# Copies of queries to the other partitions by DMA within SBUF, transfers to every second partition, and VectorE's exps in every group of the seven-tile blocks

## The chip, the cores and the metric

The kernel runs on one core of a Trainium2 chip. The metric is the device time of one launch in microseconds; a run's number is the median of several executions. The profile is of one execution and has its own time.

## What is computed

The reference is four graph layers on 3,327 nodes with 128 features; each adds its result to its input and normalizes. Nearly all the time is in layer 0, an attention with 8 heads' worth of features per slot and 128 slots. Cut to what matters:

```python
q = (x @ Wq.T).reshape(d, n, h)        # d = 128 slots, n = 3327 nodes, h = 8
k = (x @ Wk.T).reshape(d, n, h)
v = (x @ Wv.T).reshape(d, n, h)
a = jnp.einsum('dnh,dmh->dnm', q, k) * scale
a = a + adj + adj                      # the same matrix stands for both encodings
a = jax.nn.softmax(a, axis=2)
out = jnp.einsum('dnm,dmh->dnh', a, v)
```

So for every slot there is a 3,327 x 3,327 matrix of scores with a contraction over 8 features only, an exponential of each, and a product with 9 columns (8 values and a one for the sum). The other three layers are products of the adjacency matrix with 128 or 256 columns.

## The kernel before, in words

**Preparation** (to 339 us) projects x to queries, keys and values. Queries and keys are split into a high and a low part of TensorE's float32r[...]: 32 rows of contraction. They are stored in the DRAM scratches `q_s` and `k_s`, 16 rows each (8 high, 8 low), one row of all slots behind the other.

**Attention** (339 to 10,020 us) is tiled thus. There are 7 stretches of 476 queries (`CW`). For each of them the keys are taken in four parts (`KBS`): two of seven tiles of 128 keys, two of six. That makes 28 blocks. In a block the 128 slots are gone through in 32 groups of four (`GROUP`), 896 groups in all. PSUM holds the scores of one slot and block in three sets `sc0`, `sc1`, `sc2` of 3, 2 and 2 tiles (2, 2 and 2 in a six-tile block). At a block's first slot the transposed edges are put into PSUM; each further slot adds its score less that of the slot before, so the edges stay there. That is why the contraction has 64 rows: 32 for the slot's keys and queries and 32 for the earlier slot's keys (`back` = 1) and negated queries.

A group's sets have twelve places, 0 to 11: four slots, three sets each. At each place TensorE computes the set's scores (L610) and ScalarE their exps (L618). Tiles alternate between the two halves of TensorE's rows: even tiles use partitions 0 to 63 of `kt` and `qt`, odd tiles partitions 64 to 127. So `qt` holds the same queries in both halves. In three of four groups (`on_vector`) the last set of the first slot gets its exps from VectorE (`vector_exp`: L574, L575, L577 and five times L580). A group is weighed by the values (`weigh`, L636) while the next group's scores are computed. `PLACES` says after which places the tiles are weighed: for six-tile blocks one tile at every second place, for seven-tile blocks by a list of its own for each of four successive groups; `FIRST` serves the first group of a block.

Order of the work: TensorE, ScalarE, VectorE and GpSimd run in the order in which the program is written. VectorE's smaller steps go through a list `vec`, from which `vector_work` takes them by a running account of estimated microseconds (`clock`), so that they come between the sets. SP only issues loads, in order; before one it waits for the semaphores of the buffer that it overwrites and for the DMA that used the same completion semaphore last (there are eight).

At the start of group n (`prepare`), SP issues the loads for group n+2 (`load_heads`): three into `qt` (L469) and eight into `kt` (L476), both with three buffers; every second group also the values `vs` (L511), and every eighth a piece `ai` of adj (L184) for the later layers. VectorE then completes the queries of group n+1 (`copy_queries`): L499 and L500 write the negated queries of the earlier slots to partitions 32 to 63, L501 copies partitions 0 to 63 to 64 to 127. The loads put the 16 rows of `q_s` or `k_s` on 16 neighbouring partitions.

**The last layers** (10,020 us to the end) are not touched.

The functions that the diff touches, with the line numbers of the profile:

Of the kernel before, what the change touches and what calls it, by code (L numbers as in the profile page):

```python
# [19 lines left out]
P = 128  # L20
GROUP = 4
# [29 lines left out]
def kernel(ctx: ExitStack, tc: tile.TileContext, x, adj, wq, wk, wv, wo,  # L51
# [14 lines left out]
    nc = tc.nc  # L66
    N, D = x.shape
    HD = wq.shape[0]
    H = HD // D
# [175 lines left out]
    with tc.tile_pool(name="pw", bufs=1) as pw, tc.tile_pool(name="pa", bufs=2) as pa, \  # L245
# [155 lines left out]
        one = pw.tile([1, 512], F32, name="one")  # L401
        nc.vector.memset(one, 1.0)
        nc.sync.dma_start(out=klead_s, in_=zero)
        for row in (0, 2 * H):
            nc.sync.dma_start(out=klead_s[row:row + 1, :], in_=one)
        nc.sync.dma_start(out=k_s[:, SLOTS:RS], in_=zero[0:2 * H, :])

# [1 line left out]
    def attention():  # L409
        with tc.tile_pool(name="acc", bufs=1) as accp, tc.tile_pool(name="kq", bufs=3) as kq, \  # L410
# [31 lines left out]

            SETS = {7: [(0, 3), (3, 2), (5, 2)], 6: [(0, 2), (2, 2), (4, 2)]}

            def on_vector(g):

                return g % 4 != 0

            PLACES = {7: ((0, 2, 4, 4, 7, 7, 9), (0, 0, 3, 7, 7, 10, 10), (0, 0, 3, 6, 6, 9, 9), (0, 0, 3, 6, 7, 10, 10)),
                      6: ((0, 2, 4, 6, 8, 10),) * 4}

            FIRST = {7: (4, 4, 5, 7, 7, 10, 10), 6: (4, 4, 7, 7, 10, 10)}

            def load_heads(b, g):


                c0, kb = blocks[b]
                k0, nt = KBS[kb]  # L460
                ns = [(nt + 1) // 2, nt // 2]
                kt = kq.tile([P, GROUP, 4 * P], F32R, name="kt")
                qt = kq.tile([P, GROUP, CW], F32R, name="qt")
                qf = qt.bitcast(F32)
                kf = kt.bitcast(F32)

                d = g * GROUP
                for row, a, n in ((0, 0, 16), (16, H, H), (24, 0, H)):
                    nc.sync.dma_start(out=qf[row:row + n],  # L469
                                      in_=flat_ap(q_s, a * RS + c0 + d * N, [[RS, n], [N, GROUP], [1, CW]]))  # L470
                for back in range(2):
                    j = 1 if back and g == 0 else 0
                    for rg in range(2):
                        for u in range(2):
                            row = 64 * rg + 32 * back + 16 * u
                            nc.sync.dma_start(  # L476
                                out=kf[row:row + 16, j:, 0:ns[rg] * P],
                                in_=flat_ap(k_s, (d + j - back) * N + (k0 + (ns[0] if rg else 0)) * P,
                                            [[RS, 16], [N, GROUP - j], [1, ns[rg] * P]]))
                if g == 0:  # L480
                    for rg in range(2):
                        nc.sync.dma_start(out=kf[64 * rg + 32:64 * rg + 64, 0, 0:ns[rg] * P],
                                          in_=klead_s[:, 0:ns[rg] * P])
                    nc.vector.memset(qf[32:64, 0], 0.0)
                    u = c0 // SUPER
                    cut = min(CW, (u + 1) * SUPER - c0)
                    for uu, a, n in ((u, 0, cut), (u + 1, cut, CW - cut)):
                        for row, part in ((0, 0), (8, 1), (16, 1), (24, 0)):
                            if n:
                                nc.sync.dma_start(  # L490
                                    out=qf[32 + row:33 + row, 0, a:a + n],
                                    in_=flat_ap(lead_s[uu], part * SUPER + c0 + a - uu * SUPER, [[SUPER, 1], [1, n]]))
                return kt, qt

            def copy_queries(b, g):
                qt = heads[b, g][1]
                qf = qt.bitcast(F32)
                before = heads[b, g - 1][1].bitcast(F32)[0:32, GROUP - 1] if g else qf[32:64, 0]
                return [(0.9, None, lambda: nc.vector.tensor_scalar(qt[32:64, 1:], qf[0:32, 0:GROUP - 1], -1.0, None, ALU.mult)),  # L499
                        (0.4, None, lambda: nc.vector.tensor_scalar(qt[32:64, 0], before, -1.0, None, ALU.mult)),  # L500
                        (1.2, None, lambda: nc.vector.tensor_copy(qt[64:128], qf[0:64]))]  # L501

            def tile_at(nt, i):

# [41 lines left out]
            def prepare(b, d):  # L546

                n = b * NHG + d // GROUP
                if d % GROUP == 0:
                    while any(of is None for _, of, _ in vec):  # L550
                        vec.pop(0)[2]()
                    if n + 2 < len(groups):
                        heads[groups[n + 2]] = load_heads(*groups[n + 2])
                    if n + 1 < len(groups):
                        values[groups[n + 1]] = load_values(*groups[n + 1])
                    while stores:
                        store(*stores.pop(0))
                    background(n)


                if d % GROUP == 1 - on_vector(d // GROUP) and n + 1 < len(groups):
                    vec.extend(copy_queries(*groups[n + 1]))
                if d % GROUP == 3:
                    background_work(n)
# [29 lines left out]
            def exponents(b, d, si):  # L594
                kb = blocks[b][1]
                nt = KBS[kb][1]
                t0, n = SETS[nt][si]
                s = sc[si]
                if d == 0:
                    for i in range(n):  # L600
                        tl = tile_at(nt, t0 + i)[2]
                        for j, (q0, w) in enumerate(subs):
                            nc.tensor.matmul(s[:, i, q0:q0 + w], lhsT=edges[b][0:w, j, tl * P:(tl + 1) * P],
                                             rhs=ident[0:w, 0:w], is_transpose=True,
                                             start=(j == 0), stop=True, skip_group_check=True)
                kt, qt = heads[b, d // GROUP]
                k = d % GROUP
                for i in range(n):
                    rg, pos, _ = tile_at(nt, t0 + i)
                    nc.tensor.matmul(s[:, i, 0:CW], lhsT=kt[64 * rg:64 * rg + 64, k, pos * P:(pos + 1) * P],  # L610
                                     rhs=qt[64 * rg:64 * rg + 64, k, :],
                                     start=False, stop=True, skip_group_check=True)
                e = ex.tile([P, (3, 2, 2)[si], CW], F32, tag=f"e{si}", name=f"e{si}", bufs=(6, 7, 8)[si])
                if on_vector(d // GROUP) and (d % GROUP, si) == (0, 2):
                    vector_exp(e[:, 0:n, :], s[:, 0:n, 0:CW], (b, d // GROUP))
                    clock[1] += 1.2
                else:
                    nc.scalar.activation(e[:, 0:n, :], s[:, 0:n, 0:CW], AF.Exp, scale=2.0)  # L618
                for i in range(n):
                    es[b, d, t0 + i] = e[:, i, :]  # L620
                if d % (2 * GROUP) == 0 and d // (2 * GROUP) < len(subs) and si == len(SETS[nt]) - 1 \
                        and b + 1 < len(blocks):
                    load_edges(b + 1, d // (2 * GROUP))
# [39 lines left out]
            with tc.manual_schedule(engines={mybir.EngineType.PE, mybir.EngineType.Activation,  # L663
                                             mybir.EngineType.Pool, mybir.EngineType.DVE}):
                for j in range(len(subs)):
                    load_edges(0, j)
                for n in range(2):
                    heads[groups[n]] = load_heads(*groups[n])
                for _, _, step in copy_queries(*groups[0]):
                    step()  # L670
                values[groups[0]] = load_values(*groups[0])
                for b, d in steps:
                    prepare(b, d)
                    for si in range(len(SETS[KBS[blocks[b][1]][1]])):
                        vector_work(b)
                        exponents(b, d, si)
                        if queue:
                            at = PLACES[len(queue_of)][d // GROUP % 4] if d >= GROUP else FIRST[len(queue_of)]
                            for _ in range(at.count(place)):
                                weigh(*queue.pop(0))  # L680
                        place += 1
                    if d % GROUP == GROUP - 1:
                        while queue:
                            weigh(*queue.pop(0))
                        queue_of = [(b, d // GROUP, r) for r in range(KBS[blocks[b][1]][1])]
                        queue, place = list(queue_of), 0
                while queue:
                    weigh(*queue.pop(0))
                while stores:
                    store(*stores.pop(0))  # L690
# [558 lines left out]
```

## Time and profile before

| | |
|---|---|
| median of 3 runs | 10,783.05 us (10,782.16 to 10,786.95) |
| profiled execution, its own time | 10,792.99 us |
| its span | 10,791.2 us |
| TensorE (PE) busy | 10,545.2 us, 98% |
| ScalarE (ACT) busy | 9,680.6 us, 90% |
| VectorE (DVE) busy | 8,700.0 us, 81% |
| GpSimd (POOL) busy | 1,852.8 us, 17% |
| DMA packets | 995,965, 1,516.25 MB, mean 141 GB/s |
| SP's queue (q1) | 1,371.76 MB, its packets take 78.7% of 16 engines' span |

How to read it: busy time is the union of an engine's instructions. A group of instructions is given by its line, engine, operation and shapes, with count, busy time, mean duration of one, and the idle time of the engine before them with what ended it. Where instructions overlap in the engine's pipeline, the mean of one is longer than the spacing. The forty digits of a row are tenths of busy time in forty equal slices. TensorE's ends are modelled, so its 98% does not mean that it works at its peak.

### The profile page before, as it was taken

To read this page: it belongs to the slowest core of one execution; us is meant where nothing else is said; L and a number is where in the kernel's file an instruction comes from. 1 tells how busy PE (TensorE), PEld (TensorE's weight loads), DVE (VectorE), ACT (ScalarE), POOL (GpSimd) and SP (SyncE) were. 2 spreads that over 40 slices of the span, in tenths; PEclk is the share of its full clock that TensorE was granted. 3 is DMA by queue.
4 is the path that set the end of the run, shared out by engine and by line. 5 is a ranking of instruction groups with operands and counts; after the bars stand their busy time and mean duration, and the time that the engine had idled before them with its cause. 6 is when DMAs were issued, how large, how long until landed. Compare 5 with 4: busy or idle time off the path is not lost. (4 is left out here: it accounts for less than half of the span.)

```text
span 10791.2 us, 203132 instructions
## 1 busy us (share of the span) xinstructions
PE 10545.2 (98%) x76941; PEld 4103.4 (38%) x76941; DVE 8700.0 (81%) x9695; ACT 9680.6 (90%) x10559; POOL 1852.8 (17%) x2742
## 2 busy tenths in 40 slices
PE   8899999999999999999999999999999999999999
PEld 5333333333333333333333333333333333333779
DVE  6688998889988899888899788998889877788412
ACT  3799999999999999999999999999999999999400
POOL 0111122111221122211122111121112100001200
PEclk9899999999999999999999999999999999999999
DMA  7888888888888888888888788888888888888676
GB/s 251 156 129 124 131 139 136 128 126 129 136 140 125 125 132 135 137 125 128 129 139 137 116 123 122 125 132 129 129 128 126 124 120 118 115 114 121 214 281 246
DMA packets 995965, 1516.25 MB, mean 141 GB/s; under 512 B 203368, under 2 KB 813474, under 8 KB 981164
## 3 DMA queue, kind: packets, MB, share of 16 engines
q1 hardware_dynamic: 897750, 1371.76, 78.7%
q0 software_dynamic: 79616, 116.88, 4.9%
q8 instruction: 624, 10.22, 0.5%
q10 hardware_dynamic: 17620, 14.49, 0.4%
q14 instruction: 355, 2.90, 0.1%
HBM read 1371.86 MB, written 130.35 MB: 139 GB/s over the span
## 5 line engine op out<-in xcount | busy, mean ns | idle before, releaser
L618 ACT ACTIVATE e<-sc 128x952 f32<-128x952 f32 (+1 forms) x10080 | 9458.5, 1090 | 247.6 <-PE sc L610 216.5
L636 PE MATMUL o<-e,v_pad 128*32 128x476 f32 (+1 forms) x46592 | 5621.3, 573 | 38.2 <-DVE acc L649 25.5
L610 PE MATMUL sc<-qt,kt 64*128 64x476 f32 x23296 | 4470.2, 438 | 113.8 <-ACT e L618 63.6
L610 PEld LDWEIGHTS sc<-qt,kt 64*128 64x128 f32 x23296 | 2166.0, 184 | 4415.6 <-ACT e L618 3840.0
L580 DVE SCALAR_TENSOR_TENSOR e<-e,ey 128x952 f32<-128x952 f32 x2016 | 2319.7, 1151 | 66.4
L515 POOL COPY v_pad<-vs 128x192 f32<-128x192 f32 (+1 forms) x896 | 606.7, 702 | 7666.8 <-DMA vs<-v_img 5875.9
L636 PEld LDWEIGHTS o<-e,v_pad 128*32 128x32 f32 (+1 forms) x46592 | 1045.1, 108 | 1967.2 <-issue 1931.9
L574 DVE TENSOR_SCALAR ey<-sc 128x952 int32<-128x952 f32 x672 | 772.1, 1149 | 624.6 <-PE sc L610 615.1
L501 DVE CAST qt<-qt 64x1904 fp32r<-64x1904 f32 x896 | 1041.5, 1162 | 30.4
L499 DVE TENSOR_SCALAR qt<-qt 32x1428 fp32r<-32x1428 f32 x896 | 809.0, 903 | 140.4 <-DMA qt<-q_s 109.5
L234 POOL DMA_DIRECT2D adjT_s<-at x1352 | 853.5, 638 | 232.6 <-DMA adjT_s<-at 168.2
L580 DVE SCALAR_TENSOR_TENSOR e<-ey 128x952 f32<-128x952 f32 x672 | 773.5, 1151 | 23.3
L580 DVE SCALAR_TENSOR_TENSOR e<-e,et 128x952 f32<-128x952 f32 x672 | 774.1, 1152 | 20.7
L1085 PE MATMUL bank<-y,eT 128*128 128x128 f32 (+1 forms) x4056 | 473.9, 276 | 0.4 <-DVE h L1207 0.4
L1085 PEld LDWEIGHTS bank<-y,eT 128*128 128x128 f32 (+1 forms) x4056 | 465.3, 192 | 5.7 <-DVE h L1207 0.6
L577 DVE TENSOR_SCALAR ey<-ey 128x952 int32<-128x952 int32 x672 | 447.1, 665 | 23.3
L575 DVE TENSOR_SCALAR et<-ey 128x952 int32<-128x952 int32 x672 | 443.1, 659 | 22.5
L500 DVE TENSOR_SCALAR qt<-qt 32x476 fp32r<-32x476 f32 x896 | 385.7, 430 | 6.2 <-DMA qt<-lead_s 3.2
L649 DVE TENSOR_TENSOR acc<-o,acc 128x476 f32<-128x476 f32 x231 | 150.4, 651 | 248.8 <-PE o L636 247.6
L1045 ACT ACTIVATE rstd<-mv,eps 128x1 f32<-128x1 f32 x104 | 30.4, 293 | 265.2 <-DVE mv L1043 265.2
L656 POOL DMA_DIRECT2D o_s<-acc x308 | 238.7, 779 | 30.0 <-DVE acc L649 20.2
L647 DVE COPY acc<-o 128x476 f32<-128x476 f32 x77 | 50.1, 650 | 136.4 <-PE o L636 135.8
(151 smaller groups left out, 2357.8 us busy)
## 6 DMA issues: line engine op xcount, KB each, us to landing
kt<-k_s SPq DMA_DIRECT2D x5320, 96.0 KB
kt<-k_s SPq DMA_DIRECT2D x1764, 128.0 KB
eT<-adjT_s SPq DMA_DIRECT2D x78, 1664.0 KB
qt<-q_s SPq DMA_DIRECT2D x896, 119.0 KB
qt<-q_s SPq DMA_DIRECT2D x1792, 59.5 KB
vs<-v_img SPq DMA_DIRECT2D x224, 224.0 KB
adjT_s<-at POOLq DMA_DIRECT2D x1352, 32.0 KB, 6.3
vs<-v_img SPq DMA_DIRECT2D x224, 192.0 KB
```

The lines of the kernel that those rows point to most:

```text
L234: nc.gpsimd.dma_start(out=flat_ap(adjT_s, (t * P + 32 * q) * NP + c * PIECE, [[NP, 32], [P, ns], [1, P]]), in_=at[32 * i:32 * i + 32].rear ...
L499: return [(0.9, None, lambda: nc.vector.tensor_scalar(qt[32:64, 1:], qf[0:32, 0:GROUP - 1], -1.0, None, ALU.mult)), (0.4, None, lambda: nc ...
L501: (1.2, None, lambda: nc.vector.tensor_copy(qt[64:128], qf[0:64]))]
L515: nc.gpsimd.tensor_copy(vp[:, 32:32 + nt * GROUP * 32].rearrange("p (x c) -> p x c", c=32)[:, :, 0:H], vs.rearrange("p (x c) -> p x c", c=H))
L574: nc.vector.tensor_scalar(yi, x, -58 * math.log(2.0), 2 ** 24 / math.log(2.0), ALU.max, ALU.mult)
L575: vec.append((0.7, of, lambda: nc.vector.tensor_scalar(ti, yi, UPPER, EXPONENT, ALU.bitwise_and, ALU.bitwise_xor)))
L577: vec.append((0.7, of, lambda: nc.vector.tensor_scalar(yi, yi, LOWER, QUARTER, ALU.bitwise_and, ALU.bitwise_or)))
L580: vec.append((1.2, of, lambda i=i, a=a: nc.vector.scalar_tensor_tensor(e, e if i else y, a, t if i == len(POLY) - 1 else y, ALU.add, ALU.m ...
L610: nc.tensor.matmul(s[:, i, 0:CW], lhsT=kt[64 * rg:64 * rg + 64, k, pos * P:(pos + 1) * P], rhs=qt[64 * rg:64 * rg + 64, k, :], start=False ...
L618: nc.scalar.activation(e[:, 0:n, :], s[:, 0:n, 0:CW], AF.Exp, scale=2.0)
L636: nc.tensor.matmul(o[32 * j:32 * j + 32, 0:CW], lhsT=values[b, g][:m, c:c + 32], rhs=es[b, g * GROUP + j, r][:m, :], start=(r == 0 and u = ...
L1085: nc.tensor.matmul(ps[:n, 0:D], lhsT=e[:m, s, :n], rhs=y[:m, s, col:col + D], start=(s == 0), stop=(s == T - 1))
```

## The change

- The rows of `q_s` and `k_s` go to every second partition. Even partitions of a stretch of 32 take what partitions 0 to 15 took, odd ones what 16 to 31 took; the queries' low and high rows in the odd places keep their order. The rows of ones in `klead_s` and the rows for `lead_s` move along.
- The copy of `qt` to partitions 64 to 127 (L501) is no longer an instruction of VectorE but a DMA that SP issues, from partitions 0 to 63 of the same tile. In `vec` it costs nothing.
- In seven-tile blocks `on_vector` holds for every group, so VectorE computes one set's exps in all 32 groups of such a block, not in 24. Six-tile blocks stay as they are.
- `PLACES` has one list for all groups of a seven-tile block.

```diff
-        for row in (0, 2 * H):
+        for row in (0, 1):
             nc.sync.dma_start(out=klead_s[row:row + 1, :], in_=one)
...
-            def on_vector(g):
+            def on_vector(nt, g):
 
-                return g % 4 != 0
+                return nt == 7 or g % 4 != 0
...
-            PLACES = {7: ((0, 2, 4, 4, 7, 7, 9), (0, 0, 3, 7, 7, 10, 10), (0, 0, 3, 6, 6, 9, 9), (0, 0, 3, 6, 7, 10, 10)),
-                      6: ((0, 2, 4, 6, 8, 10),) * 4}
+            PLACES = {7: (1, 1, 4, 6, 8, 10, 10), 6: (0, 2, 4, 6, 8, 10)}
...
-                for row, a, n in ((0, 0, 16), (16, H, H), (24, 0, H)):
-                    nc.sync.dma_start(out=qf[row:row + n],
+                for row, a, n in ((0, 0, 2 * H), (1, H, H), (1 + 2 * H, 0, H)):
+                    nc.sync.dma_start(out=qf[row:row + 2 * n - 1:2],
                                       in_=flat_ap(q_s, a * RS + c0 + d * N, [[RS, n], [N, GROUP], [1, CW]]))
...
-                            row = 64 * rg + 32 * back + 16 * u
+                            row = 64 * rg + 32 * back + u
                             nc.sync.dma_start(
-                                out=kf[row:row + 16, j:, 0:ns[rg] * P],
+                                out=kf[row:row + 31:2, j:, 0:ns[rg] * P],
...
-                        for row, part in ((0, 0), (8, 1), (16, 1), (24, 0)):
+                        for row, part in ((0, 0), (16, 1), (1, 1), (17, 0)):
...
-                        (1.2, None, lambda: nc.vector.tensor_copy(qt[64:128], qf[0:64]))]
+                        (0.0, None, lambda: nc.sync.dma_start(out=qf[64:128], in_=qf[0:64]))]
```

The three calls of `on_vector` and `PLACES` are fitted to this.

More of the change, by code (lines that the diff above doesn't have):

```diff
@@ L558, in prepare @@
                     background(n)
-                if d % GROUP == 1 - on_vector(d // GROUP) and n + 1 < len(groups):
+                if d % GROUP == 1 - on_vector(KBS[blocks[b][1]][1], d // GROUP) and n + 1 < len(groups):
                     vec.extend(copy_queries(*groups[n + 1]))
@@ L613, in exponents @@
                 e = ex.tile([P, (3, 2, 2)[si], CW], F32, tag=f"e{si}", name=f"e{si}", bufs=(6, 7, 8)[si])
-                if on_vector(d // GROUP) and (d % GROUP, si) == (0, 2):
+                if on_vector(nt, d // GROUP) and (d % GROUP, si) == (0, 2):
                     vector_exp(e[:, 0:n, :], s[:, 0:n, 0:CW], (b, d // GROUP))
@@ L677, in attention @@
                         if queue:
-                            at = PLACES[len(queue_of)][d // GROUP % 4] if d >= GROUP else FIRST[len(queue_of)]
+                            at = PLACES[len(queue_of)] if d >= GROUP else FIRST[len(queue_of)]
                             for _ in range(at.count(place)):
```

## The prediction

> **What bounds the kernel now.** First the page: its busy shares and its forty slices.
>
> ```profile
> PE 10545.2 (98%) x76941; PEld 4103.4 (38%) x76941; DVE 8700.0 (81%) x9695; ACT 9680.6 (90%) x10559; POOL 1852.8 (17%) x2742
> ...
> ACT  3799999999999999999999999999999999999400
> ...
> DMA  7888888888888888888888788888888888888676
> ```
>
> The attention runs from 339 to 10,020 us, 90% of the time, with ScalarE (ACT) and TensorE (PE) full and the DMA engines at 0.8. Which engine ends a group of four slots is read from one seven-tile block and one six-tile block, the groups of instructions with their shapes kept apart. First the seven-tile block (window 3101 to 3468), then the six-tile one (3837 to 4158):
>
> ```profile
> L618 ACT ACTIVATE e<-sc 128x952 f32<-128x952 f32 x232 | 217.2, 1003 | 3.4 <-PE sc L610 3.2
> ...
> L618 ACT ACTIVATE e<-sc 128x1428 f32<-128x1428 f32 x128 | 179.8, 1405 | 0.6 <-PE sc L610 0.6
> ...
> L501 DVE CAST qt<-qt 64x1904 fp32r<-64x1904 f32 x32 | 37.4, 1169 | 1.1
> ```
>
> ```profile
> L618 ACT ACTIVATE e<-sc 128x952 f32<-128x952 f32 x360 | 312.0, 1031 | 10.1 <-PE sc L610 10.1
> ```
>
> The column after the second bar is idle time. In the seven-tile block ScalarE idles 4.0 of 367 us: it is the bound. The mean durations overlap, so the spacing is computed: in the six-tile block (321 - 10.1)/360 = 0.864 us for a 952-column exp; then (363 - 232 x 0.864)/128 = 1.27 us for a 1428-column one. A seven-tile group with all twelve sets on ScalarE needs 4 x 1.27 + 8 x 0.864 = 11.99 us, one whose set goes to VectorE 11.13. Cutting the trace at the starts of L618 gives 11.97 for g%4 = 0 and 11.24, 11.59, 11.19 for 1, 2, 3; the 11.59 has 0.31 us of ScalarE waiting for PE, a matter of PLACES. Six-tile groups take 9.95 us with VectorE's set against 9.5 of ScalarE's work: there PE paces (a load run and a weigh run start every 1.57 us at best, six per group, and 0.5 us more is lost).
>
> The third view is SP's own waits:
>
> ```profile
> SPq L469 <- PE sc L610: 2811.0, 845, 7.9
> SPq L476 <- DMA qt<-q_s: 925.1, 1376, 4.0
> ```
>
> SP waits for PE to leave a buffer, issues eleven loads, and the later ones wait for earlier ones to land. By the semaphores' times the last kt load lands 10.7 to 11.9 us after the first issue, in groups of 9.9 to 11.6 us: harmless two groups ahead, but DMA has little left.
>
> [...]its packet records show 1,536-byte packets (kt) at 65 ns for the fastest tenth, medians of 161 to 189 and the slowest tenth at 252 to 265 ns, four times the fastest. [...]SP waits for VectorE's L499 and L500.
>
> **The change part by part.** (1) The CAST L501 goes: 896 x 1.16 = 1,041 us of VectorE, 1.16 per group. None is on the path of a seven-tile block; in six-tile blocks PE's weight loads wait 0.4 to 0.8 us per group for VectorE's L574, mostly under running matmuls, so I give 0.05 x 336 = 17 us, bounds 0 and 50.
>
> (2) In place of it 896 DMAs of 64 x 7,616 B = 487 KB: 437 MB on top of 1,516. SP issues each in 0.3 to 0.4 us, behind the loads of group n+2. Packet records give one engine 24 B/ns (1,904 bytes in 78 ns); 30.5 KB each is 1.25 us[...]. Landing adds about 1.2 us (the fastest tenth of the tiny lead_s loads). So 2.5 to 3.7 us from the head of the ring to landing.
>
> (3) Striding: kt and qt packets should come down from a mean of 2.7 times the fastest to 1.5, bounds 1.3 and 2.7. kt is some 0.59 of the engines' time, qt 0.11, of 0.87; the share falls to about 0.55, and the copy adds 0.11 to 0.22: 0.66 to 0.77, below today's.
>
> (4) VectorE's exps in all groups of fourteen seven-tile blocks: 112 more, each 1.15 + 2 x 0.66 + 5 x 1.15 = 8.22 us (rows L574 to L580), 921 us in all. Per seven-tile group VectorE then has 8.22 + 0.91 + 0.43 for the queries, 0.22 for acc and 0.63 for the background: 10.4 against 11.13. It fits at 93%. In the groups with the background's 2.4 us it runs about 1 us late; L574 may then delay PE, cost 0 to 0.3 us there.
>
> (5) ScalarE loses 8 exps of 0.86 per block: 6.9 us. (6) The new PLACES open with two tiles at place 1 and weigh in five runs. By the shortest spacings in the trace (two weighed tiles 1.74 us, one 0.94, score runs of 7, 7, 5, 4, 5 tiles 1.06, 1.06, 0.84, 0.62, 0.84) PE needs 10.7 per group, under ScalarE's 11.13, as the g%4 = 3 pattern does today at 11.19. So all groups come near 11.2; g%4 = 2 gains 0.4 x 8 = 3.2 us.
> The other edits, of klead_s, lead rows and on_vector's argument, move no work: zero.
>
> Seven-tile blocks: 6.9 + 3.2 = 10.1 us less the slips of (4), 8 x 0.15 = 1.2: 8.9, and some of it lost where a group starts late: 8, times 14 = 112 us gained; bounds 50 and 140.
>
> (7) The new wait. PE's first odd tile of group n+1 needs qt's upper half; every later matmul stands behind it. From the first load's issue to that matmul the trace has 9.85 to 10.07 us in six-tile blocks and 11.1 to 11.6 in seven-tile ones. The copy's landing: eleven issues at 0.42 = 4.6, the ring drained of kt at 5.5 to 6.5, vs every second group 1 us, the copy 1.9 to 2.5, landing 1.2: 8.6 to 11. In seven-tile groups it is hidden; in six-tile groups with vs or with an ai piece (some 240 of 448) it is at the edge. I take 0.2 us x 240 = 48 us, bounds 0 and 400. Behind SP's wait stand only the next group's loads, which wait for PE anyway.
>
> Sum: -112 - 17 + 48 = -81 us. Against the profiled execution's own 10,793 (span 10,791) this is 10,712; the median of the runs is 10 us lower, so **10,702 us**.
>
> **The rivals.** *Slower: the copy lands late.* If striding brings packets only to twice the fastest, the ring is drained of kt and qt near 7 us, vs at 8, and the copy lands at 11 to 11.7: in six-tile groups 1 to 1.7 us after PE wants it. At 0.6 us on average over 448 groups, 269 - 112 = 157 us more: 10,940. It decides from 0.25 us on average, where 448 x 0.25 eats the gain. For it: the kt landings show a ring that is nearly full. Against it: the packets' fourfold spread[...].
>
> *Striding does nothing*[...]: kt still lands at 11 us, the copy at 14; groups stretch by 4 and 3 us, 448 x 7 = 3,100 us: 13,900. The full rate of some packets of the same size speaks against it.
>
> *No gain:* VectorE's exps come late in every seven-tile group, PE waits for L574 and ScalarE for PE, 0.8 us per group in a quarter of them, with half of (7): 112 - 90 - 24 leaves nothing, 10,780. VectorE's 35.0 us of waiting for PE at L574 per block speaks against it.
>
> **How the numbers follow.** Chance 0.57 for the forecast, 0.31 for the late copy, 0.02 for striding without effect, 0.10 for no gain. A measurement here can tell 0.2%, 22 us, from no change. Of the no-gain case 0.06 lies within that and 0.02 on each side: faster 0.59, same 0.06, slower 0.35. Range: below, 140 + 50 gained and nothing lost would be 10,593, so 10,605; above, the late copy's 10,940 is taken in: 10,950. As cases of both signs hold most of the chance: the forecast's own range is 10,605 to 10,760.
>
> **What would show it.** Right: L501's group gone; L618 at 8 fewer exps per seven-tile block, 9,968 in all; seven-tile blocks near 360 us (now 368); DMA digits at 7, not 8; 1,536-byte packets near 100 ns; hardly any wait of PE or its weight loads at L610 for DMA qt<-qt. Wrong: such waits in hundreds of us, six-tile blocks longer than their 321 to 325 us, DMA digits at 9, or PE's waits for DVE ey L574 grown from 153 us to several hundred.

## The result, and the profile after

The changed kernel takes 12,242.6 us (median of 4 runs, 12,223.8 to 12,260.7) against 10,784.1 us (4 runs): ratio 1.1351, 95% interval [1.1337, 1.1365]. It is 13.5% slower, 1,458 us, where 81 us less had been forecast. The profiled execution took 12,260.7 us, its span is 12,258.9.

Four lines of the page, in the same order as those shown of before (engines, slices), and the line of SP's DMA queue:

```profile
PE 11148.8 (91%) x76941; PEld 4172.1 (34%) x76941; DVE 8584.1 (70%) x9695; ACT 9658.3 (79%) x10447; POOL 1801.7 (15%) x2742
...
ACT  3888878887788888888878888878888889988600
...
DMA  7655565555555655655555555555555555555576
...
q1 hardware_dynamic: 969430, 1808.55, 55.3%
```

ScalarE's digits are down from 9 to 8 and 7: it is no longer full. The DMA engines are at 5 and 6 although SP's queue moves 1,808.55 MB, 437 more. So the first half of the idea came out as forecast. By the packet records the 1,536-byte packets of kt have a median of 65 ns where it was 161 to 189; 65 ns was the fastest tenth before. That the stride relieves the DMA engines e1 shows below; by what mechanism it shortens the packets no run shows.

Groups of instructions with their shapes apart, a seven-tile block (3,533 to 3,939 us) and then a six-tile one (4,346 to 4,739 us); the columns are count, busy time and mean, and idle time with its releasers:

```profile
L620 ACT ACTIVATE e<-sc 128x952 f32<-128x952 f32 x224 | 210.0, 1002 | 0.1
L620 ACT ACTIVATE e<-sc 128x1428 f32<-128x1428 f32 x128 | 178.0, 1391 | 49.4 <-PE sc L612 49.4
L612 PE MATMUL sc<-qt,kt 64*128 64x476 f32 x896 | 176.8, 441 | 29.5 <-DMA qt<-qt 23.5 <-DMA qt<-q_s 6.0
```

```profile
L620 ACT ACTIVATE e<-sc 128x952 f32<-128x952 f32 x360 | 316.4, 999 | 77.9 <-PE sc L612 77.8
L612 PE MATMUL sc<-qt,kt 64*128 64x476 f32 x768 | 163.5, 468 | 45.8 <-DMA qt<-qt 17.3 <-issue 15.0 <-DMA qt<-q_s 13.5
```

ScalarE has its eight exps fewer in the seven-tile block (224 for 232), but it idles 49.5 us there and 77.9 us in the six-tile block, where it idled 4.0 and 10.1. It waits for TensorE's scores, and TensorE for `DMA qt<-qt`, the new copy. In the whole span the waits name the same (columns: total us, times, longest; the first line is of before, the others of after):

```profile
ACT e L618 <- PE sc L610: 216.5, 589, 4.8
```

```profile
ACT e L620 <- PE sc L612: 1703.3, 1662, 15.2
...
PE sc L612 <- DMA qt<-qt: 445.8, 258, 15.2
PE sc L612 <- DMA qt<-q_s: 377.9, 145, 6.0
PEld sc L612 <- DMA qt<-qt: 365.7, 171, 15.6
```

The two lines of `qt<-qt` make 811 us; a stop of TensorE and one of its weight loads can overlap in this sum. The stops that the profile puts down to `qt<-q_s` end in the same way as those of `qt<-qt`: by the semaphores' times TensorE's first odd tile starts 0.04 to 0.24 us after the copy has landed. Counted so, TensorE stands still for the copy in 515 of 894 groups, 993 us in sum.

Why is the copy late? SP issues it, so I read SP's timeline (start, duration, line, how many):

```profile
4052.07 2.03 SPq L471 DMA_DIRECT2D qt<-q_s  x3
4054.14 5.05 SPq L478 DMA_DIRECT2D kt<-k_s  x8
4059.30 0.52 SPq L513 DMA_DIRECT2D vs<-v_img  x1
4059.92 0.52 SPq L503 DMA_DIRECT2D qt<-qt  x1
4063.46 2.02 SPq L471 DMA_DIRECT2D qt<-q_s  x3
4065.52 5.70 SPq L478 DMA_DIRECT2D kt<-k_s  x8
4071.26 2.04 SPq L184 DMA_DIRECT2D ai<-in_adj_dram  x4
4073.41 0.53 SPq L503 DMA_DIRECT2D qt<-qt  x1
```

The eleven loads take 7.1 to 7.8 us of issuing, not 4.6; then a vs load (0.5) or four pieces of ai (2.0) come ahead of the copy, which is issued 7.9 us after the group's first load in the first case and 10.0 us in the second. From its issue to its landing it needs another 4.5 us (median by the semaphores), where 2.5 to 3.7 had been forecast: about 1.2 us to its first packet, 2.6 us of packets and 0.5 us more. The counterpart of before, same columns:

```profile
4057.55 1.02 SPq L469 DMA_DIRECT2D qt<-q_s  x3
4058.61 5.21 SPq L476 DMA_DIRECT2D kt<-k_s  x8
```

These 5.21 us contain waits for earlier loads (the prediction's L476 <- DMA qt<-q_s). What one issue takes is seen in the answer for the source line, of before and of after (min/median/max in ns):

```profile
L476 SPq DMA_DIRECT2D kt<-k_s x7168: 302/420/2400, 322.6 to 9993.8; - x200
```

```profile
L478 SPq DMA_DIRECT2D kt<-k_s x7168: 555/593/2142, 320.1 to 11458.8; - x200
```

The shortest issue of a kt load went from 302 to 555 ns, that of a qt load (L469, L471) from 264 to 559. The form of the destination was the only change to these instructions. Group by group, from the first qt load's issue (medians): the copy is issued after 7.5 us in plain groups, 8.1 with vs and 9.7 with ai, and lands after 11.9, 12.7 and 15.0 us. TensorE's first odd tile starts within 0.25 us of the landing in 78 to 91% of the groups with vs or ai and in 36 to 48% of the plain ones. A late copy also delays what follows: TensorE leaves its old buffers later, and SP's next qt loads wait for that (L471 <- PE sc L612: 3,363.9 us in 883 waits, before 2,811.0 in 845). Blocks of both kinds stretch:

| sum of 14 blocks, us | six-tile | seven-tile |
|---|---|---|
| before | 4,514 (322 each) | 5,167 (369) |
| after | 5,485 (392) | 5,660 (404) |

The two differences, 971 and 493 us, are the whole loss. One more number belongs here: the mean granted clock of TensorE is 0.950, where it was 0.994. The clock records show 1,223 us at half clock, before 126.

### The profile page after: what moved, and what is told of

Read it like the earlier page. It is cut to its first block, busy times and chain, and to the rows that moved or that the text cites. A ratio compares the mean times of both kernels' runs of the same rounds, so it can differ in the third digit from the quotient of the medians.

```text
span 12258.9 us, 204931 instructions
## 1 busy us (share of the span) xinstructions
PE 11148.8 (91%) x76941; PEld 4172.1 (34%) x76941; DVE 8584.1 (70%) x9695; ACT 9658.3 (79%) x10447; POOL 1801.7 (15%) x2742
## 3 DMA queue, kind: packets, MB, share of 16 engines
q1 hardware_dynamic: 969430, 1808.55, 55.3%
## 5 line engine op out<-in xcount | busy, mean ns | idle before, releaser
L638 PE MATMUL o<-e,v_pad 128*32 128x476 f32 (+1 forms) x46592 | 5968.1, 600 | 4.3 <-DVE acc L651 0.9
L612 PE MATMUL sc<-qt,kt 64*128 64x476 f32 x23296 | 4769.1, 454 | 1015.7 <-DMA qt<-qt 445.8
L612 PEld LDWEIGHTS sc<-qt,kt 64*128 64x128 f32 x23296 | 2237.8, 191 | 5768.0 <-ACT e L620 3611.5
L582 DVE SCALAR_TENSOR_TENSOR e<-e,ey 128x952 f32<-128x952 f32 x2352 | 2708.6, 1152 | 77.6
L576 DVE TENSOR_SCALAR ey<-sc 128x952 int32<-128x952 f32 x784 | 901.4, 1150 | 2267.1 <-PE sc L612 2229.1
L517 POOL COPY v_pad<-vs 128x192 f32<-128x192 f32 (+1 forms) x896 | 694.6, 793 | 9397.6 <-DMA vs<-v_img 7471.1
L582 DVE SCALAR_TENSOR_TENSOR e<-ey 128x952 f32<-128x952 f32 x784 | 902.6, 1151 | 27.2
L582 DVE SCALAR_TENSOR_TENSOR e<-e,et 128x952 f32<-128x952 f32 x784 | 905.1, 1154 | 22.2
L501 DVE TENSOR_SCALAR qt<-qt 32x1428 fp32r<-32x1428 f32 x896 | 818.9, 914 | 63.7 <-DMA qt<-q_s 44.4
L234 POOL DMA_DIRECT2D adjT_s<-at x1352 | 763.0, 573 | 22.4 <-issue 18.9
L577 DVE TENSOR_SCALAR et<-ey 128x952 int32<-128x952 int32 x784 | 518.5, 661 | 26.6
L579 DVE TENSOR_SCALAR ey<-ey 128x952 int32<-128x952 int32 x784 | 518.1, 661 | 27.1
L1047 ACT ACTIVATE rstd<-mv,eps 128x1 f32<-128x1 f32 x104 | 30.5, 293 | 266.9 <-DVE mv L1045 266.9
L1190 PE MATMUL bank<-a,y 128*128 128x512 f32 (+2 forms) x364 | 145.5, 561 | 0.0
```

Source lines behind the costliest of these rows:

```text
L234: nc.gpsimd.dma_start(out=flat_ap(adjT_s, (t * P + 32 * q) * NP + c * PIECE, [[NP, 32], [P, ns], [1, P]]), in_=at[32 * i:32 * i + 32].rear ...
L517: nc.gpsimd.tensor_copy(vp[:, 32:32 + nt * GROUP * 32].rearrange("p (x c) -> p x c", c=32)[:, :, 0:H], vs.rearrange("p (x c) -> p x c", c=H))
L576: nc.vector.tensor_scalar(yi, x, -58 * math.log(2.0), 2 ** 24 / math.log(2.0), ALU.max, ALU.mult)
L577: vec.append((0.7, of, lambda: nc.vector.tensor_scalar(ti, yi, UPPER, EXPONENT, ALU.bitwise_and, ALU.bitwise_xor)))
L579: vec.append((0.7, of, lambda: nc.vector.tensor_scalar(yi, yi, LOWER, QUARTER, ALU.bitwise_and, ALU.bitwise_or)))
L582: vec.append((1.2, of, lambda i=i, a=a: nc.vector.scalar_tensor_tensor(e, e if i else y, a, t if i == len(POLY) - 1 else y, ALU.add, ALU.m ...
```

## The experiments

"Theory A" in the expectations is that a strided issue occupies SP longer, so that the copy, last in SP's order, comes too late. The other letters: F, the new PLACES are to blame; G, what is left is SP's queue being nearly full; H, TensorE's whole work bounds the seven-tile group; L, one stretch of that group does. B, C and D are explained where they stand. Ratios are to the kernel before, measured beside each.

**One part alone.** `e1_stride_only` is before with nothing but the rows on every second partition:

```diff
-                for row, a, n in ((0, 0, 16), (16, H, H), (24, 0, H)):
-                    nc.sync.dma_start(out=qf[row:row + n],
+                for row, a, n in ((0, 0, 2 * H), (1, H, H), (1 + 2 * H, 0, H)):
+                    nc.sync.dma_start(out=qf[row:row + 2 * n - 1:2],
...
-                                out=kf[row:row + 16, j:, 0:ns[rg] * P],
+                                out=kf[row:row + 31:2, j:, 0:ns[rg] * P],
```

> The kernel before with nothing but the rows on every second partition (kt, qt, klead_s and lead rows); L501 stays VectorE's CAST, exps and PLACES as before. Theory A (the stride itself makes SP's issues longer): the median kt issue is near 0.59 us as after the change, not 0.42; eleven issues take about 7.3 us, which is hidden two groups ahead, so the time is 10,784 within 0.5%. Theory B (the copy within SBUF on the same queue makes all issues longer): kt issues stay at 0.42, the time is the same or up to 0.5% shorter. Both: 1,536-byte packets fall from a mean of 170 to 190 ns to about 90, DMA busy from 0.86 to about 0.5.

Measured: 10,777.5 us, ratio 0.9991 [0.9982, 1.0000]. The same lines as above, slices and the source line of the kt loads:

```profile
DMA  7544454445554454544455444454444444444676
```

```profile
L476 SPq DMA_DIRECT2D kt<-k_s x7168: 555/593/2061, 318.9 to 9980.2; - x200
```

The DMA engines fall from 8 to 4 and 5 tenths for the same bytes (q1's 1,371.76 MB take 45.9% of 16 engines' span, before 78.7%), and the kernel is not faster: the transfers were hidden. The issue's 555/593 ns are there without the copy and without anything late. So the stride itself makes them long. SP's issues, with the short gaps between them, then fill about 8 of some 10 us per group, where they filled 5.3; in e1, where nothing with a deadline stands behind them, that costs nothing.

`e2_copy_only` is before with nothing but the copy as a DMA:

```diff
-                        (1.2, None, lambda: nc.vector.tensor_copy(qt[64:128], qf[0:64]))]
+                        (0.0, None, lambda: nc.sync.dma_start(out=qf[64:128], in_=qf[0:64]))]
```

> The kernel before with L501 as a DMA that SP issues, nothing else; rows stay on neighbouring partitions. Theory A: kt issues stay at 0.42 us; but the ring is full of kt[...], so the copy lands 12 to 14 us after the first load's issue, and groups stretch to that: 12,500 to 13,500, worse than the whole change. Theory B: kt issues at 0.59 without any stride. A rival, that the copy is harmless and the exps or PLACES made the change slow, expects 10,784 or less.

Measured: 13,654.2 us, ratio 1.2657 [1.2636, 1.2678]. Issues are short again (kt median 419 ns), but the copy needs 7.6 us from issue to landing (median), and groups take 13 to 15 us. This is the state that the rival "striding does nothing" assumed, and its 13,900 us came within 2%. The copy alone costs 26.6%; in the whole change, with the stride, the loss is 13.5%.

**The copy taken out again.** `e3_cast_back` is the changed kernel with L503 as VectorE's copy (`nc.vector.tensor_copy(qt[64:128], qf[0:64])`, in `vec` still at 0.0).

> The changed kernel with the copy back on VectorE (same place in the list, account 0), so striding, exps in all seven-tile groups and the new PLACES stay. If the copy's landing is what PE waits for (theory C): the waits for DMA qt<-qt are gone, six-tile blocks return to about 322 us, seven-tile blocks are set by VectorE with 10.4 + 1.16 = 11.6 us a group, 370 to 380 us; 10,790 to 10,950. If exps or PLACES cost the time (theory D): still over 12,000. kt issues: 0.59 under A, 0.42 under B.

Measured: 11,076.4 us, ratio 1.0269 [1.0252, 1.0286]; the clock is back at 0.995. So the copy's DMA accounts for 1,166 of the 1,458 us. In what is left TensorE's weight loads wait for VectorE; seven-tile groups take 11.5 to 12.1 us:

```profile
PEld sc L612 <- DVE ey L576: 745.8, 673, 5.4
```

With 1.16 us of CAST on top of the 10.4 us counted in step (4) VectorE needs 11.6 us per seven-tile group, by this sum more than ScalarE's 11.13, so that the exps in every group would not fit beside the copy. That is an estimate: `vec` still counts the copy at nothing, so VectorE's order is not that of before. Half of the loss is not the exps', since the six-tile blocks, where VectorE has no more of them than before, take 4,662 us for 4,514; the order of `vec` may be the reason, which no run tests.

**The copy earlier.** `e4_ahead` completes the queries of group n+2, not n+1, from the third slot of group n:

```diff
-                if d % GROUP == 1 - on_vector(KBS[blocks[b][1]][1], d // GROUP) and n + 1 < len(groups):
-                    vec.extend(copy_queries(*groups[n + 1]))
+                if d % GROUP == 2 and n + 2 < len(groups):
+                    vec.extend(copy_queries(*groups[n + 2]))
```

> The changed kernel with the queries of group n+2, not n+1, completed in group n (from its third slot on), so that the copy has one more group to land; both first groups are completed ahead of the loop. Nothing is left out. Theory C: waits of PE for the copy vanish, seven-tile blocks near 360 us and six-tile blocks near 322 us, 10,650 to 10,750, faster than before; the granted clock returns from 0.95 to 0.99. Theory D, or a queue that is too slow as such (12 issues of 0.6 us and up to five more in one group): still 11,500 to 12,200.

Measured: 11,100.5 us, ratio 1.0288 [1.0271, 1.0305]. TensorE and its weight loads wait 49 us in sum for the copy, no longer 811. But VectorE now stands before loads that have not landed, with its exps queued behind, and SP before VectorE's negations, with the next loads queued behind (the waits, VectorE's and then SP's):

```profile
DVE qt L501 <- DMA qt<-q_s: 669.4, 127, 12.1
```

```profile
SPq L503 <- DVE qt L502: 953.4, 501, 7.5
```

The wait was exchanged for smaller ones. `e5_ahead_places` is e4 with the seven-tile list (0, 0, 3, 6, 7, 10, 10) that before used for g%4 = 3.

> The copy one group ahead as in e4, and for seven-tile blocks the list (0, 0, 3, 6, 7, 10, 10), which was one of four before, in place of (1, 1, 4, 6, 8, 10, 10). In e4 a seven-tile group's usual length is 11.36 us where ScalarE has 11.13 of work: after two tiles weighed at place 1 TensorE brings the three-tile set of place 3 only 2.6 us into the group, and ScalarE stands still for about 0.5. If that is the new PLACES' doing (theory F): seven-tile groups go to about 11.2, 100 us less than e4, near 11,000; six-tile blocks as in e4. If VectorE's exps in all groups do it, it stays at 11,100.

Measured: 11,110.4 us, 1.0297 [1.0280, 1.0314], no difference: the new list is not to blame, and theory F falls. `e8_ahead_pool` is e5 with the copy issued by GpSimd (`nc.gpsimd.dma_start`), from the fourth slot on.

> As e5 with the queries completed from the fourth slot on and the copy issued by GpSimd, not SP, so that SP has one issue less in a group and never waits for VectorE. Theory G: six-tile blocks return to 321 to 325 us, and the time to 10,650 to 10,800, faster than before or equal to it. If VectorE's or TensorE's own work in the changed blocks holds the time, it stays near e5.

Measured: 10,959.9 us, 1.0161 [1.0144, 1.0178]: 150 us less than e5, with two edits at once (queue and slot), so it doesn't say which of them it is.

**The copy ahead of the key loads.** `e6_copy_first` leaves every DMA and its form as it is and moves the completion of group n+1, the copy and VectorE's two negations ahead of it, to between the qt and the kt loads of group n+2. So the copy comes earlier in SP's order, and the negations come at the start of the group in VectorE's:

```diff
+                for _, _, step in between:
+                    step()
                 for back in range(2):
...
-                        heads[groups[n + 2]] = load_heads(*groups[n + 2])
+                        heads[groups[n + 2]] = load_heads(*groups[n + 2], copy_queries(*groups[n + 1]))
+                        clock[1] += 1.3
...
```

> The changed kernel with the completion of group n+1's queries, copy included, placed between the three qt loads and the eight kt loads of group n+2, so that in SP's queue only three issues and not eleven stand ahead of the copy; PLACES and exps as changed. Theory C with the place in the queue as its cause: the copy is issued 2 to 3 us after the first load and lands at 7, PE's waits for it are gone, and the time falls by 1,000 us or more, to 11,000 to 11,200, with what e4 leaves (PLACES, and SP's queue of 8 to 11 us of issues per group). If it is the copy's own 4.5 us whatever its place, less than 300 us are won.

Measured: 10,907.7 us, ratio 1.0112 [1.0095, 1.0129]. The same 896 copies with the same strided loads cost 1,335 us less. With e3 and e4, where TensorE's wait for the copy goes too, this settles the cause. SP's timeline, and then the waits for the copy:

```profile
4053.22 2.02 SPq L471 DMA_DIRECT2D qt<-q_s  x3
4055.34 0.53 SPq L505 DMA_DIRECT2D qt<-qt  x1
4055.92 6.20 SPq L480 DMA_DIRECT2D kt<-k_s  x8
4062.62 2.23 SPq L471 DMA_DIRECT2D qt<-q_s  x3
```

```profile
PE sc L615 <- DMA qt<-qt: 33.3, 18, 9.4
...
PEld sc L615 <- DMA qt<-qt: 9.9, 1, 9.9
```

The copy is issued 2.1 us after the group's first load, where it was 7.9, and TensorE and its weight loads wait 43 us in sum for `DMA qt<-qt`, where it was 811. The seven-tile blocks now take 5,153 us in sum (before 5,167), the six-tile ones 4,637 (before 4,514): the rest of the loss lies in the six-tile blocks. In the group shown kt ends at 4,062.12 and the next group begins at 4,062.62, so SP is busy for all but half a microsecond. Its queue was the next suspect, and e9 tests it.

`e7_copy_first_places`, e6 with the list of e5:

> As e6, and with the list (0, 0, 3, 6, 7, 10, 10) for seven-tile blocks. Theory F: 80 to 130 us less than e6 (10,900 to 11,050). If SP's queue of issues now sets the pace (theory G: eleven loads at 0.63 us from start to start, vs, ai and the copy are 8 to 10 us of a six-tile group's 9.95), six-tile blocks stay above 330 us and the time above 10,850.

Measured: 10,936.1 us, 1.0137 [1.0120, 1.0154], 28 us more than e6: the seven-tile blocks take 5,183 us. The old list does not make the new exps cheaper, so F falls here too.

`e9_first_gp` is e6 with the loads of vs and ai issued by GpSimd (`nc.gpsimd.dma_start`), which relieves SP's queue without any change to kt and qt.

> As e6, with the loads of ai and vs issued by GpSimd, so that SP issues only qt, the copy and kt in a steady group. In e6 SP's issues fill 9.9 us of a six-tile group, and the six-tile blocks are longer (331 to 337 us) just while ai pieces are loaded, 320 to 323 us after the last piece. Theory G (SP's queue has become the bound): all six-tile blocks at 320 to 324 us, seven-tile blocks at 366 to 367: 10,740 to 10,790, level with before. If the copy or VectorE hold the six-tile blocks, it stays near 10,900.

Measured: 10,846.6 us, 1.0062 [1.0049, 1.0076]: 61 us less than e6, but not the 10,740 to 10,790 expected. Six-tile blocks have 4,580 us, still 66 more than before. Relieving SP's queue (theory G) takes away about half of what e6 had left. The trace says where most of the other half lies: 45 of the 66 us are in the last group of the six-tile blocks, which takes 13.8 us on average, where it took 10.3. In e6 it takes 15.8 us, 72 of the 123 us. There VectorE stands before L504 until the rows for the next block's first slot (`lead_s`) have landed, its exps are queued behind, and TensorE waits for their first step (L579); in these groups of e6 ScalarE idles 68 us for TensorE's scores, before 5. VectorE's waits at L504, of e6 and then of e9 (before has one, of 3.2 us, at its L500):

```profile
DVE qt L504 <- DMA qt<-lead_s: 76.0, 28, 6.2
```

```profile
DVE qt L504 <- DMA qt<-lead_s: 53.8, 25, 4.8
```

So by these waits e6's own edit causes this part, as it puts the negations ahead of VectorE's exps; no run moves them back for a block's first group. The excess also fades with the ai pieces: the last of them is loaded in the eleventh of the fourteen six-tile blocks, the twelfth still takes 325 to 326 us in e6 and e9, where it took 322.4, and the last two take 320 to 323 in both, as before.

**Is the stride needed?** `e10_first_old_exps` is e6 with before's exps (`on_vector` without `nt == 7 or`) and before's four lists; `e11_first_no_stride` is e10 with the rows on neighbouring partitions.

> As e6, with VectorE's exps and PLACES of the kernel before (three of four groups in seven-tile blocks): striding and the copy stay. It prices the eight more exps of a block. The three groups with VectorE's set averaged 11.34 us before, as e6's do now, the fourth 11.97: theory H, a group that gives a set to VectorE wins 0.6 us and not 0.86, since TensorE cannot bring the next set at once; so e10 is 8 x 0.6 = 5 us a seven-tile block slower than e6: 10,940 to 11,000. By the prediction's step it would be 10 us a block, 11,050; if the exps gain nothing, 10,907 or less.

> As e10, with the rows on neighbouring partitions again: the copy by DMA ahead of the kt loads, no stride, everything else as before the change. SP's issues are short (kt 0.42 us), but [...]DMA was 0.87 busy before, and the copy adds 0.15 or more. [...]loads land late, and the time is 11,300 to 12,500, slower than e10 in spite of the shorter issues. If place in the queue is all, it is 10,790 to 10,850.

Measured: 10,921.2 us, 1.0125 [1.0110, 1.0141], and 11,224.7 us, 1.0404 [1.0377, 1.0431]. Without the stride the DMA engines are at 9 tenths, with it at 6 and 7, and SP's kt loads wait (the slices of e10, of e11, and SP's wait in e11):

```profile
DMA  7666676666666666666667666666666666566676
```

```profile
DMA  7999999999999999999999899889999999999776
```

```profile
SPq L481 <- DMA qt<-qt: 964.6, 575, 4.3
```

L481 is a kt load that waits for the copy to land; in e6 the same wait is 15.9 us in sum. So the stride is worth 2.8% once the copy is there, although its longer issues cost SP's time. And e10 against e6 prices the new exps with their list: the seven-tile blocks take 5,166 us in e10 and 5,153 in e6, 1 us per block, where 8 had been forecast; the totals differ by 14 us, and their intervals overlap.

**Why the exps bring so little.** In e6 the steady seven-tile group (the median) takes 11.36 us, not 11.13 to 11.2. Two kernels on e6 each leave out one tile's weighing, the same amount of TensorE's work, at different places: `e12_first_less_weigh` tile 3 (`for j in range(GROUP if r != 3 else 0)`), `e13_first_less_early` tile 1.

> As e6, but one tile of every group (r = 3) is not weighed: of a group's TensorE work 0.8 us is left out, and that part of the attention's sum is missing; scores, exps, loads and copies are all there. The question is what holds a seven-tile group with VectorE's set at 11.36 us whatever PLACES says. Theory H (TensorE does, with what it loses at each change between scores and weighing): the steady seven-tile group (third of four) falls from 11.36 to ScalarE's own 11.1, steady six-tile groups from 9.86 to 9.4 or less. If ScalarE or VectorE holds them, they stay at 11.36 and 9.86.

> As e12, but the tile left out of the weighing is r = 1, the second of the two that TensorE weighs at place 1 of a seven-tile group (that part of the attention's sum is missing). If the stretch from place 0 to place 3 is what holds the group (theory L), TensorE brings place 3 0.8 us earlier, at most when ScalarE has let go of the set (1.45 us into the group): ScalarE's pause there shrinks from 0.45 to 0 or 0.15 and the steady group from 11.37 to 11.1 or 11.2. If it is something else it stays at 11.37.

Measured: 10,895.9 us, 1.0101 [1.0084, 1.0118], and 10,755.4 us, 0.9969 [0.9958, 0.9980]. With tile 3 left out the steady group stays at 11.37 us; with tile 1 it takes 11.10, and ScalarE has no idle time in it. TensorE's sum does not bound the group (H falls); the order does (L). Two tiles weighed at place 1 stand ahead of the scores of places 2 and 3; place 2 is VectorE's, so ScalarE goes straight on to place 3, whose exp starts 2.56 us into the group in e6 and 2.30 in e13 (medians).

Four kernels tried to use this on e9 by other lists alone, with all of the sum computed. `e15_first_gp_late7`: seven-tile (3, 3, 5, 6, 8, 10, 10). `e14_first_gp_late`: the same and six-tile (3, 3, 5, 7, 9, 10). `e16_first_gp_one4`: (1, 4, 4, 6, 8, 10, 10). `e17_first_gp_spread`: (1, 4, 6, 7, 8, 10, 10).

> As e9 (copy ahead of kt, ai and vs loaded by GpSimd), with the list (3, 3, 5, 6, 8, 10, 10) for seven-tile blocks: no tile is weighed before place 3. Theory L: steady seven-tile groups 11.15, 0.2 us x 448 = 90 us less than e9: 10,755, just under before (10,787). Otherwise 10,847 or more.

> As e15, and (3, 3, 5, 7, 9, 10) for six-tile blocks, where ScalarE pauses in the same way for place 3 (0.5 us). Theory L for six-tile groups: 9.86 goes to 9.5, up to 120 us less than e15: 10,640 to 10,700. But TensorE has little room there (9.40 us of work in the shortest spacings), and the pause may only move: then as e15.

> As e9 with one edit: PLACES of seven-tile blocks (1, 4, 4, 6, 8, 10, 10), so one tile and not two is weighed ahead of the three-tile scores of place 3, and two at place 4; all of the sum is computed. Theory L (the stretch from place 0 to place 3, shortened by leaving a tile out in e13, sets the seven-tile group): the pause before place 3 goes, but two tiles at place 4 put one of some size before place 6 or 5, since place 3's exp of three tiles is 1.27 us and PE needs 1.74 for two weighed tiles and 0.84 for the next scores. Steady seven-tile group between 11.2 and 11.5, total 10,800 to 10,880. Rival (only TensorE's amount of work counts, not its order): same as e9, 10,846 within 15.

> As e9 with one edit: PLACES of seven-tile blocks (1, 4, 6, 7, 8, 10, 10), five single tiles and one pair, so that no pause before place 3 is left and none is put elsewhere, at the price of one more change between loading and weighing per group. Theory L: steady seven-tile group 11.15 to 11.25 for 11.36, 448 x 0.15 = 67 us less, total 10,770 to 10,800. Rival (TensorE's amount of work counts): one more run of weighed tiles adds about 0.1 us per group, total 10,860 to 10,900.

| | ratio, interval | steady seven-tile group, us |
|---|---|---|
| e9 | 1.0062 [1.0049, 1.0076] | 11.36 |
| e15 | 1.0599 [1.0585, 1.0614] | 12.4 |
| e14 | 1.0813 [1.0798, 1.0828] | as e15; six-tile 10.6, where e9 has 9.8 |
| e16 | 1.0205 [1.0188, 1.0222] | 11.73 |
| e17 | 1.0328 [1.0310, 1.0345] | 12.06 |

All four are misses in the total. In e16 and e17 the pause at place 3 goes, just as L says: its exp starts 2.20 us into the group, where it is 2.57 in e9. But the exp of place 5 then starts 0.6 us later than ScalarE's work would let it in e16, and those of places 6 and 9 some 0.4 us each in e17; in e15 the pause moves to place 4. So L names the pause rightly, and moving tiles in these ways only moved it. No version that computes the whole sum beats the kernel before; e1 is level with it.

## Why the prediction was wrong

**Step (7), the new wait, failed.** The rest is smaller. Its sum had three terms, and all came out too small. The first was the start of the copy. The text had "eleven issues at 0.42 = 4.6" and let the copy begin when the ring is drained, after 5.5 to 6.5 us, 1 us later with vs. But the eleven issues alone take 7.1 to 7.8 us, so SP issues the copy only after 7.5 us (median), 8.1 with vs. 0.42 us was read from the page of before, from contiguous loads, and carried over to strided ones; e1 shows 593 ns (kt) and 671 ns (qt) for the same loads with the stride alone. The second was the copy's own time, 3.1 to 3.7 us with its landing in this sum, 4.5 measured. The 3.7 has 2.5 us of packets, twice the 1.25 that 30.5 KB take at the 24 B/ns read from before; the factor of two no trace showed. The third was the order: the text saw that the copy stands behind vs and ai in SP's queue, but gave ai nothing of its own, where four issues take 2.0 us and the copy starts at 9.7. So a landing forecast for 8.6 to 11 us, where TensorE wanted it at 9.85 to 11.6, came at 11.9 to 15.0, and what was priced at 48 us, at most 400, cost 1,335 (after less e6).

The price of a late copy was too small as well. It was put on 240 six-tile groups, with the argument "Behind SP's wait stand only the next group's loads, which wait for PE anyway." In the trace this is a loop: loads, copy, TensorE, and then the next loads, which wait for TensorE. The median six-tile group takes 12.0 to 12.1 us, the copy's landing in plain groups 11.9. TensorE is also granted less clock (0.950); how much of the 1,335 us that is the runs don't separate.

**The rival "the copy lands late"** had the mechanism, and the sign that decided. It went wrong in the cause of the lateness, which it saw in packets that stay slow, and hence in size: 0.6 us in 448 groups, where six-tile groups became 2.2 us longer (70 us per block of 32 groups) and the seven-tile groups, held to be safe, 1.1 us. "Wrong: such waits in hundreds of us, six-tile blocks longer than their 321 to 325 us" is what the profile then showed.

**Step (3), striding, was right**: the 1,536-byte packets' mean is 91 ns, 1.4 times the fastest tenth, where 1.5 times was forecast, which no trace of before showed, and the DMA digits in e6, which is nearly as short as before, are 6 for a forecast share of 0.66 to 0.77. It bought nothing by itself (e1), and without it the copy costs 2.8% more (e11).

**Step (1) was right** in that the CAST was not on the path of the seven-tile blocks: with it gone and the exps and lists of before (e10) they take 5,166 us, before 5,167. The 17 us that it gave the six-tile blocks can hardly be seen: in the last two blocks of e6 they take 322.6 and 320.1 us, in the same blocks of before 322.9 and 321.3, where 1.2 us each had been forecast.

**Steps (4) to (6) were mis-sized.** 8 us per seven-tile block were forecast, 1 us came (e10 against e6). The text read the future floor from g%4 = 3, 11.19 us, and from TensorE's sum of 10.7. In steady groups, by medians, before has 11.80, 11.22, 11.51 and 11.07 us for g%4 = 0 to 3, on average 11.40, and e6 has 11.36 to 11.37 in all four. So the groups g%4 = 0 and 2 gain 0.43 and 0.15 us, and the other two lose 0.14 and 0.30: some 0.04 us per group are left, about 1 us per block. The fast g%4 = 3 owed its time to its place in the cycle and not to its list alone, for in e7 all groups have that list and take 11.35. e13 shows what holds 11.36 up: a pause of ScalarE behind two weighed tiles.

**What stays open:** by what mechanism the stride shortens the packets; why a strided issue takes SP 0.25 to 0.3 us longer at the shortest, and why the issues of unchanged loads behind them become longer too; how much of the loss is TensorE's lower clock; and what a kernel like e9 would take if a block's first queries were completed later.

## What to carry to other kernels

Here a transfer was late by the sum of what its queue did before it (7.5 to 9.7 us ahead of a copy of 4.5): price every issue ahead of it in the form that it will have after the change, and put the one transfer with a deadline ahead of those that are wanted two groups later (e6: 1,335 us less). The access pattern that relieved the DMA engines (8 tenths to 4 and 5 in e1) loaded the engine that issues (0.42 us for a kt load to 0.59), so look at both before calling a transfer hidden. What the transfer itself waits for moved with it (76.0 us of VectorE's waits at L504 in e6, before 3.2), so look for the groups where that comes late. And a floor is read from the mean of a whole cycle of groups (11.40 us before), not from the best one of it (11.07).

## What was not expected of the hardware

- An issue on SP of a load with 16 rows takes 0.59 us (median, kt) with the rows on every second partition and 0.42 with neighbouring ones, 0.555 and 0.302 at the shortest (e1 against before). Behind such loads even an unchanged vs load takes 0.523 us (median), where it took 0.338; that too is so with the stride alone.
- In e6 the second kt issue behind the copy takes 1.78 us (median of 894 groups), the others of these loads 0.59 to 0.60. Whether that is a wait or the issue itself the profile does not tell.
- The copy within SBUF, 64 rows of 7,616 B, needs 4.5 us from issue to landing (median; 4.3 in e6) with the DMA engines at 5 to 6 tenths; its packets have a mean of 513 ns and a fastest tenth of 290.
- With stops of TensorE in more than half of the groups its mean granted clock is 0.950, where it was 0.994; in e2, with longer stops, it is 0.904, and with the copy in time (e6) 0.989.
